# Seven places between the stages of a graph layer rearranged

## Chip, cores and metric

One Trainium2 chip; the kernel runs on 1 core. The metric is the device time in microseconds of one execution. An engine carries out its own instructions in order, and waits on semaphores for what the others deliver. The engines are TensorE (PE), VectorE (DVE), ScalarE (ACT) and GpSimd (POOL); SyncE (SP) issues most of the transfers.

## The reference

The input is 32 graphs of 512 nodes with 256 features, and an adjacency matrix for each. Cut to what matters:

```python
h = jnp.maximum(_layernorm(x, axis=-1), 0.0)
# the layer, on h:
c = relu(bn1(conv1d(hc, conv1_w)))                     # 1 tap, hc: h with channels in front
x_conv = relu(bn2(conv1d(c, conv2_w, pad 8)) + hc)     # 17 taps
s = h @ w_se.T + b_se                                  # 3 numbers a node
A = jnp.exp(-dist(s)) * adj
msg = relu(h @ w_msg.T + b_msg)
x_nmp = einsum('bnm,bmd->bnd', A, msg)
gi = concatenate([x_conv, x_nmp]) @ w_ih.T + b_ih
gh = h @ w_hh.T + b_hh
r, z = sigmoid(gi_r + gh_r), sigmoid(gi_z + gh_z)
nn_ = tanh(gi_n + r * gh_n)
out = x + (1 - z) * nn_ + z * h
```

## The kernel before, in words

All is float32. The 32 graphs are worked through in two groups of 16 (GB). For each group there are two stages, and after both groups a third runs over pairs of graphs. Almost everything stands under `tc.manual_schedule()`, where each engine gets its instructions in the order in which the program issues them; tiles in a few rotating buffers (`bufs=`) add the waits for a buffer.

**First stage** (`first_part`), once for each group, a loop over its graphs: load x (`load_x`), layer norm (`statistics`: bn_stats on DVE, the power of -1/2 on POOL, L398; `normalise`: four chunks of 128x256, L411 on DVE or L409 on ACT), transposes on PE into phT (L419) and relu into hT (L423), the first convolution (`conv1`, pc, L439; the bias is added on DVE into h, L442, relu on ACT, L443), and a transform of windows to a frequency-like domain (px, L454). In group 0 the weights of the second convolution are transformed in between (`weights_to_freq`, pw, L363; ACT or DVE copies them out to wst, SP stores them to wd). `between(b)` hands out these 32 transforms, two in an iteration, three in two of them (L1306). In group 1 the fronts of the loop carry the last four products of group 0, the `left` list (L1440 on), which `fill()` issues one entry at a time, and the sums that prepare the gates' weights (`combine`), whose first entry is a load of w_hhT by four transfers issued on POOL (L211).

**Node stage** (`nodes`), once for each group, a loop over the graphs in the order `todo`: 15, 14, 0, 1, ..., 13 in group 0. It has, for each graph, messages (`message`: products pm, L558, adds on DVE into st and msg, L560 and L561, relu on ACT, L565), features and their factors (`features`: fl and fr on ACT, L573 to L575; `factors`: two transposes psl and psr on PE, L580 and L584, copied by ACT to sl and sr, L582 and L587), exponents (`exponents`: pd, L604, exp on ACT, L610), the mask (`turn` transposes adj on DVE, L593; `masked`, L614), sums of blocks on POOL (`block_sums`, L641: ms, msg, ts, A, ms, ts, ms, ts) and the aggregation with seven products in place of eight (`aggregate7`, L666, adds on DVE at L680 to L686; `save_nmp` stores the result by SP). In between stand the products of the second convolution in the frequency domain, by units (`multiply(u)`, `product`, py, L503): re and im parts by PE, and for most units a third product of `both` (L483) and `wsum` (L470), which POOL prepares two units ahead (`prepare`; two buffers each). Group 0 has 36 units in its node stage over 16 graphs, so that an iteration has two or three (`mine`); the last has three: 33, 34 and 35. The last four units, 36 to 39, are the left-over ones.

**Third stage**, 16 pairs of graphs: `inverse` (back from the frequency domain, pc, L874, result in cp), gates r and z by 26 products with sums of operands (`gates_rz26`, pg, L911) and the third gate (`gate_n`, L928). The sums of operands are made by `block_sum` (L808 and L810) on POOL; for pair 0 they stand in `FIRST_ORDER`, the `hn` parts before `inverse(0)` and the `c` parts mixed in from index `ahead`, the first `c` entry. Only that one, ('t4', 'c'), is done by DVE; ('r5', 'c') follows it.

Of the kernel before, what the change touches and what calls it, by code (L numbers as in the profile page):

```python
# [12 lines left out]
AF = mybir.ActivationFunctionType  # L13
# [149 lines left out]
def gnn_layer(  # L163
# [15 lines left out]
    nc = tc.nc  # L179
# [5 lines left out]
    NC = N // P  # L185
    G = 3 * D
    W = N // V
    GB = P // W
# [44 lines left out]
    at, cols, n = {}, {}, 0  # L233
# [163 lines left out]
        nc.vector.tensor_scalar(rstd, mv[:, :, 1], LN_EPS, None, op0=ALU.add)  # L397
        nc.gpsimd.tensor_tensor(rstd, rstd, minus_half[:, :NC], op=ALU.pow)  # L398

    def normalise(b, by_scalar=False):  # L400
        mv, rstd = STATS.pop(b)
        XN[b] = pools["first"].tile([P, NC, D], FP, tag="xn", name=f"xn_{b}", bufs=2)
        if by_scalar:
            shift = work.tile([P, NC], FP, tag="shift", name=f"shift_{b}")
            nc.vector.scalar_tensor_tensor(shift, mv[:, :, 0], -1.0, rstd, op0=ALU.mult, op1=ALU.mult)
        for c in range(NC):
            dst, src = by_half(XN[b][:, c, :]), halves(X[b][:, c, :])
            if by_scalar:
                nc.scalar.activation(dst, src, AF.Identity, bias=shift[:, c : c + 1], scale=rstd[:, c : c + 1])  # L409
            else:  # L410
                nc.vector.tensor_scalar(dst, src, mv[:, c, 0:1], rstd[:, c : c + 1], op0=ALU.subtract, op1=ALU.mult)  # L411
        del X[b]
# [125 lines left out]
    def by_chunks(b):  # L538
        HQ[b] = work.tile([P, DC, N], FP, tag="hq", name=f"hq_{b}", bufs=2)
        for ic in range(DC):  # L540
            nc.scalar.copy(chunks(HQ[b][:, ic, :]), by_chunk(HT[b][:, ic, :]))
        del HT[b]

    SQ = {}

    def message(b, halves=range(2)):
        if 0 in halves:
            ST[b] = pools["nodes"].tile([P, NC, NS + 1], FP, tag="st", name=f"st_{b}", bufs=2)
            MSG[b] = pools["nodes"].tile([P, NC, D], FP, tag="msg", name=f"msg_{b}", bufs=3)
        hq = HQ[b]  # L550
        h = NC // 2
        for c0 in (h * k for k in halves):
            m = MSG[b][:, c0 : c0 + h, :]
            for j in range(h):
                c = c0 + j
                p = bank(f"pm_{b}_{c}")
                for ic in range(DC):
                    nc.tensor.matmul(p[:, : D + NS], hq[:, ic, c * P : (c + 1) * P], wmsg[:, ic, :],  # L558
                                     start=(ic == 0), stop=(ic == DC - 1))
                nc.vector.tensor_add(ST[b][:, c, :NS], p[:, D : D + NS], bmsg[:, D:])  # L560
                nc.vector.tensor_add(m[:, j, :], p[:, :D], bmsg[:, :D])  # L561
            if c0 > 0:
                SQ[b] = work.tile([P, NC, NS], FP, tag="sq", name=f"sq_{b}")
                nc.scalar.activation(SQ[b], ST[b][:, :, :NS], AF.Square)
            nc.scalar.activation(m, m, AF.Relu)  # L565
        if 1 in halves:
            del HQ[b]

# [222 lines left out]
    def block_sum(p, name, part):  # L791
        if name in BLOCK_SUMS:
            x, op, y = BLOCK_SUMS[name]
            dst, x, y = (operand(p, v, part) for v in (name, x, y))
            op = ALU.add if op == "+" else ALU.subtract
        else:
            rows = list(PAIR_SUMS)

            def whole(v):
                if isinstance(v, int):  # L800
                    return CP[p][:, v] if part == "c" else HN[p][:, :, v]
                return TNC[0][:, rows.index(v)] if part == "c" else TN[0][:, rows.index(v)]

            (x, y), op = PAIR_SUMS[name], ALU.subtract
            dst, x, y = whole(name), whole(x), whole(y)
            if part == "hn":
                for k in range(2):
                    nc.gpsimd.tensor_tensor(dst[:, k], x[:, k], y[:, k], op=op)  # L808
                return
        (nc.vector if (p, name, part) == (0, *FIRST_ORDER[ahead]) else nc.gpsimd).tensor_tensor(dst, x, y, op=op)  # L810

    def sums_ahead(p, part):
        for name in SUMS_AHEAD:
# [349 lines left out]
    def first_part(g, freq, between, left=()):  # L1163
# [15 lines left out]
            bn1_row(1, shift1, ones, diags)  # L1179
        if b0 not in STATS:  # L1180
            statistics(b0)
        normalise(b0)
        if g == 0:
            scale_w1()
            shift_w1()
# [11 lines left out]
        transpose_h(b0)  # L1197
        statistics(b0 + 1)
        fill()
        normalise(b0 + 1, g > 0)  # L1200
        if g > 0:
            statistics(b0 + 2)
        fill()
# [80 lines left out]
    with tc.tile_pool(name="freq", bufs=1) as fpool:  # L1284
# [3 lines left out]
        with phase("first", "gen"):  # L1288
            gen = pools["gen"]
            per = N // D  # L1290
            steps = [partial(weights_to_freq, gen, pc, i) for pc in range(QI // PI) for i in range(0, PI, per)]

            X[0] = pools["first"].tile([P, NC, D], FP, tag="x", name="x_0", bufs=3)
            for queue, c0, c1 in ((nc.sync, 0, 1), (nc.scalar, 1, 2), (nc.sync, 2, NC)):
                queue.dma_start(X[0][:, c0:c1, :], x[0, c0 * P : c1 * P, :].rearrange("(c p) d -> p c d", p=P))
            load_w1()
            load_x(1)
            load_taps(gen, 0, nc.sync)
            nc.sync.dma_start(taps, nc.inline_tensor(taps_np, name="dft_taps").ap())
            nc.sync.dma_start(fwd, nc.inline_tensor(fwd_np, name="dft_fwd").ap())  # L1300

            def between(b):
                if 1 <= b <= len(load_weights):
                    load_weights[b - 1]()

                n = (2, 0, *(3 if b in (6, 11) else 2 for b in range(2, GB)))[b]  # L1306
                mine = [[steps.pop(0)] for _ in range(n)]
                if b % 2 == 0 and b // 2 + 1 < QI // PI:
                    mine[b > 0].insert(0, partial(load_taps, gen, b // 2 + 1))
                return (mine[0], mine[1:]) if b == 0 else mine  # L1310

            with tc.manual_schedule():
                xf = first_part(0, freq_tile, between)
# [4 lines left out]
        def nodes(g, xf, units, last, following=()):  # L1318
# [29 lines left out]
            features(todo[0])  # L1348
            for step in message_sums(todo[0]):
                step()  # L1350
            message(todo[1], [0])
            factors(todo[0])
            by_chunks(todo[2])
            message(todo[1], [1])
            features(todo[1])
# [8 lines left out]
            for i, b in enumerate(todo):  # L1364
                mine = spread(units, i, last) if i < last else []
                more = todo[i + 1 : i + 5]
                seven = i <= last

                def bring():
                    if len(more) > 1:  # L1370
                        message(more[1])
                        features(more[1])

                def ahead():
                    if len(more) > 2:
                        load_adj(more[1], i % 2)
                    if len(more) > 3:
                        load_h(more[3])

                if len(more) == 2:  # L1380
                    load_adj(more[1], i % 2)
                flush()
                if g + 1 < NG and i == GB // 2:
                    load_x(b1)
                if g + 1 < NG and i == 3 * GB // 4:
                    statistics(b1)
                if i > 0:
                    ahead()
                if more:
                    factors(more[0])  # L1390
                if i == 0:
                    bring()
                for u in mine[:1]:
                    multiply(u)
                if i == 0:
                    ahead()
                if i > 0:
                    bring()
                if not seven:
                    aggregate(b, [0])  # L1400
                if more:
                    turn(more[0], [0, 1])
                    exponents(more[0])
                    masked(more[0], [0, 1])
                for u in mine[1:2]:
                    multiply(u)
                if more:
                    turn(more[0], [2, 3])
                    masked(more[0], [2, 3])
                if seven:  # L1410
                    aggregate7(b)
                else:
                    aggregate(b, [1])
                if len(more) > 2:
                    by_chunks(more[2])
                stores.append(partial(save_nmp, b))
                for u in mine[2:]:
                    multiply(u)
                if more and i + 1 <= last:
                    block_sums(more[0])  # L1420
            flush()

        with phase("pw", "ahead"):
# [3 lines left out]
            with phase("first", "sums"):  # L1427
                combine = combine_weights()

                def between(b):  # L1430

                    if b == GB - 3:
# [6 lines left out]
                pw, (u0, u1, u2, u3) = pools["pw"], range(UNITS - LEFT, UNITS)  # L1439
                left = [[partial(load_unit, 0, u2, pools["sums"]), partial(prepare, pw, 0, u1, xf)],  # L1440
                        [partial(product, pw, 0, u0, xf), partial(prepare, pw, 0, u2, xf)],
                        [partial(product, pw, 0, u1, xf), partial(load_unit, 0, u3), *combine.pop(0)],
                        [partial(prepare, pw, 0, u3, xf), partial(product, pw, 0, u2, xf)],
                        [partial(product, pw, 0, u3, xf)]]
                prepare(pw, 0, u0, xf)
                with tc.manual_schedule():
                    xf = first_part(1, freq_tile, between, left)
# [95 lines left out]
```

## Time and profile before

| | us |
|---|---|
| median of 3 runs | 1733.82 |
| all runs | 1733.5, 1733.82, 1737.73 |
| the profiled execution | 1737.52 |
| its span, first to last instruction | 1735.70 |

| stage | roughly, us of the span |
|---|---|
| first stage, group 0 | 0 to 161 |
| node stage, group 0 | 161 to 427 |
| first stage, group 1 | 427 to 544 |
| node stage, group 1 | 544 to 822 |
| third stage | 822 to 1736 |

A profile page gives, for each engine, its busy time and share of the span; a timeline gives start, duration, engine, line, operation and what it reads and writes, and in brackets how long the engine stood idle before and who released it. `128x512 f32` is partitions x elements. The chain of waits is the work that ended last, followed back. A wait listed as `PE py L503 <- POOL both L483` is one of PE at line 503 that ended when POOL had made `both`. In the table of stretches the columns are start and end, length, busy time (and instructions) of PE, its weight loads, DVE, ACT and POOL, then PE's granted clock, the transfers' share and GB/s.

### The profile page before, as it was taken

The numbers are of one execution on the slowest core, as the hardware profiler recorded it, in microseconds if no ns is written. First come the engines' busy times: TensorE is split into PE (matmuls) and PEld (weight loads), VectorE is DVE, ScalarE is ACT, GpSimd is POOL, SyncE is SP. The second block draws the span as 40 slices with busy tenths as digits, with TensorE's granted clock in tenths as the row PEclk, the third lists the DMA queues.
The fourth block names the chain that finished last, engine by engine and source line by source line (L and its number), as shares of the span: only waits on it lengthen the run. The fifth ranks groups of instructions, "written<-read, shape, count | busy, mean of one in ns | idle before, by whom it ended". The sixth has DMA issues, their size and how long they took to land.

```text
span 1735.7 us, 24321 instructions
## 1 busy us (share of the span) xinstructions
PE 1718.5 (99%) x7920; PEld 1323.0 (76%) x7920; DVE 1300.2 (75%) x2599; ACT 692.6 (40%) x1671; POOL 1086.8 (63%) x1071
## 2 busy tenths in 40 slices
PE   9999999999999999999999999999999999999998
PEld 6667888888898888886877787777877787778754
DVE  7785877777995667766587778777887788777867
ACT  4557555553446555554313232223223231323221
POOL 3341787777654677777767556765666556755551
PEclk9999999999999999999999999999999999999999
DMA  9988978975777988788523453245423552345323
GB/s 256 296 282 250 272 219 240 262 223 180 256 268 211 265 245 257 219 251 297 150 74 75 107 127 107 70 79 128 118 71 67 128 128 76 76 104 127 106 59 73
DMA packets 311682, 295.08 MB, mean 170 GB/s; under 512 B 147436, under 2 KB 241164, under 8 KB 311172
## 3 DMA queue, kind: packets, MB, share of 16 engines
q1 hardware_dynamic: 301588, 265.17, 55.7%
q0 software_dynamic: 6960, 26.65, 4.8%
q10 hardware_dynamic: 3008, 1.72, 0.3%
q8 instruction: 63, 1.03, 0.2%
q14 instruction: 63, 0.52, 0.1%
HBM read 194.31 MB, written 99.16 MB: 169 GB/s over the span
## 4 chain that ended last, share of the span: by engine, by line
PE 93%; DVE 2%; POOL 2%; DMA 1%; ACT 1%; SPq 1%; issue 1%; POOLq 0%; DVEq 0%; ACTq 0%
PE pg L911 29%; PE pn L928 17%; PE py L503 11%; PE pn L666 10%; PE pm L558 6%; PE pc L439 5%; PE px L454 3%; PE pc L874 3%; PE pd L604 2%; PE pw L363 2%; PE phT L419 1%; PE pg L928 1%; PE pz L928 1%; PE pc L877 1%; POOL tn L808 0%
## 5 line engine op out<-in xcount | busy, mean ns | idle before, releaser
L470 POOL TENSOR_TENSOR wsum<-wt 128x512 f32<-128x512 f32 x66 | 94.5, 1432 | 99.6 <-DMA wt<-wd 65.7
L503 PE MATMUL py<-wt,xf 128*128 128x256 f32 x640 | 154.2, 384 | 0.0
L911 PE MATMUL pg<-te,sw 128*128 128x256 f32 x600 | 154.0, 379 | 0.0
L902 ACT ACTIVATE rz<-rz,brz 128x256 f32<-128x256 f32 x180 | 86.4, 504 | 149.2 <-DVE rz L917 149.2
L503 PEld LDWEIGHTS py<-wt,xf 128*128 128x128 f32 x640 | 117.1, 190 | 34.9 <-issue 20.5
L911 PEld LDWEIGHTS pg<-te,sw 128*128 128x128 f32 x600 | 114.0, 190 | 15.5
L911 PE MATMUL pg<-hn,sw 128*128 128x256 f32 x480 | 123.2, 379 | 0.0
L911 PE MATMUL pg<-tn,sw 128*128 128x256 f32 x480 | 123.2, 379 | 0.0
L614 DVE TENSOR_TENSOR A<-A,at 128x512 f32<-128x512 f32 x124 | 116.2, 975 | 6.3 <-ACT A L610 2.7
L928 PE MATMUL pn<-tn,sw_n 128*128 128x512 f32 x256 | 120.3, 592 | 0.0
L439 PE MATMUL pc<-w,hT 128*128 128x256 f32 x512 | 119.2, 386 | 0.8 <-DVE hT L423 0.8
L1073 ACT ACTIVATE pn<-nt,vech 128x512 f32<-128x512 f32 x45 | 31.1, 692 | 217.8 <-DVE nt L1070 138.5
L558 PE MATMUL pm<-wmsg,hq 128*128 128x259 f32 x512 | 117.3, 381 | 0.0
L439 PEld LDWEIGHTS pc<-w,hT 128*128 128x128 f32 x512 | 95.9, 192 | 24.9 <-issue 8.0
L808 POOL TENSOR_TENSOR tn<-hn 128x512 f32<-128x512 f32 x64 | 86.2, 1367 | 35.7 <-PE pn L928 35.6
L558 PEld LDWEIGHTS pm<-wmsg,hq 128*128 128x128 f32 x512 | 96.6, 190 | 14.6
L911 PEld LDWEIGHTS pg<-hn,sw 128*128 128x128 f32 x480 | 91.1, 190 | 18.3 <-PE pn L928 3.3
L911 PEld LDWEIGHTS pg<-tn,sw 128*128 128x128 f32 x480 | 91.2, 190 | 12.4
L917 DVE TENSOR_TENSOR ct<-pg,ct 128x256 f32<-128x256 f32 x180 | 74.6, 415 | 32.9 <-PE pg L911 23.7
L398 POOL TENSOR_TENSOR rstd<-rstd,minus_half 128x4 f32<-128x4 f32 x32 | 33.3, 1042 | 103.0 <-DVE rstd L397 98.5
L928 PEld LDWEIGHTS pn<-tn,sw_n 128*128 128x128 f32 x256 | 48.6, 190 | 61.2 <-issue 50.5
L928 PE MATMUL pn<-hn,sw_n 128*128 128x512 f32 x192 | 90.3, 592 | 0.0
(232 smaller groups left out, 4385.4 us busy)
## 6 DMA issues: line engine op xcount, KB each, us to landing
wt<-wd SPq DMA_DIRECT2D x80, 512.0 KB, 6.3
adj<-in_adj_dram SPq DMA_DIRECT2D x128, 256.0 KB, 5.9
wd<-wst SPq DMA_DIRECT2D x64, 320.0 KB, 5.5
yd<-y SPq DMA_DIRECT2D x76, 256.0 KB, 5.0
hd<-hT SPq DMA_DIRECT2D x32, 512.0 KB, 4.4
nd<-nmp SPq DMA_DIRECT2D x32, 512.0 KB, 2.9
xb<-in_x_dram SPq DMA_DIRECT2D x128, 128.0 KB, 6.0
out_dram<-xb SPq DMA_DIRECT2D x122, 128.0 KB, 2.8
```

Source lines behind the costliest of these rows:

```text
L439: nc.tensor.matmul(p[:, j, :], HT[b][:, ic, c * P : (c + 1) * P], w1[:, ic, :], start=(ic == 0), stop=(ic == DC - 1))
L454: nc.tensor.matmul(p[:, j * 2 * L : (j + 1) * 2 * L], H1[b][:, c0 + j, ic * P : (ic + 1) * P], fwd, start=True, stop=True)
L470: nc.gpsimd.tensor_tensor(t, WT[g, u][:, 0], WT[g, u][:, 1], op=ALU.add)
L503: nc.tensor.matmul(dst, v[:, ic, :], w[:, ic, :], start=(ic == 0), stop=(ic == DC - 1))
L558: nc.tensor.matmul(p[:, : D + NS], hq[:, ic, c * P : (c + 1) * P], wmsg[:, ic, :], start=(ic == 0), stop=(ic == DC - 1))
L614: nc.vector.tensor_mul(A[b][:, mc, :], EXP.pop((b, mc)), AT.pop((b, mc)))
L666: nc.tensor.matmul(bk, left[:, k, :], right[:, k, :], start=(first and k == 0), stop=(k == 1), skip_group_check=True)
L808: nc.gpsimd.tensor_tensor(dst[:, k], x[:, k], y[:, k], op=op)
L902: nc.scalar.activation(at(dst), at(src), AF.Sigmoid, bias=brz[:, o : o + 1], scale=sign)
L911: nc.tensor.matmul(bk, SW["hk"][:, k, s, :], c if k == 2 else hn[:, k], start=(onto is None and k == 0), stop=(k == K3 - 1), skip_group_ch ...
L917: nc.vector.tensor_tensor(at(dst), at(x), at(y), op=op)
L928: nc.tensor.matmul(bk[:, t], weight(q, k, o), terms[k][q][:, t], start=(first and i == 0), stop=(i == len(ks) - 1), skip_group_check=True)
```

## The change

Seven places, all of them an order or an engine; no arithmetic is changed.

1. `normalise` takes a list of chunks for ACT instead of yes or no. Graph 0 (the first of group 0) gives it chunks 2 and 3; group 1 gives all, as before, where it gave all.
2. `between` in group 0: the iterations with a third weight transform are 12 and 14 instead of 6 and 11.
3. At the head of `nodes`, the relu of the first half of the second graph's messages is issued after the factors of the first graph.
4. In the first iteration of `nodes`, the first half of the third graph's messages is issued before `factors` of the second graph (its relu with it); second half and features after.
5. In the last iteration of `nodes`, the third unit's products come before `aggregate7` instead of after. Only group 0 has units there.
6. `left`: the load of w_hhT goes from the third entry to the last.
7. `block_sum`: DVE does the first two `c` sums of pair 0 instead of one.

```diff
@@ -397,7 +397,7 @@
         nc.vector.tensor_scalar(rstd, mv[:, :, 1], LN_EPS, None, op0=ALU.add)
         nc.gpsimd.tensor_tensor(rstd, rstd, minus_half[:, :NC], op=ALU.pow)
 
-    def normalise(b, by_scalar=False):
+    def normalise(b, by_scalar=()):
         mv, rstd = STATS.pop(b)
         XN[b] = pools["first"].tile([P, NC, D], FP, tag="xn", name=f"xn_{b}", bufs=2)
         if by_scalar:
@@ -405,7 +405,7 @@
             nc.vector.scalar_tensor_tensor(shift, mv[:, :, 0], -1.0, rstd, op0=ALU.mult, op1=ALU.mult)
         for c in range(NC):
             dst, src = by_half(XN[b][:, c, :]), halves(X[b][:, c, :])
-            if by_scalar:
+            if c in by_scalar:
                 nc.scalar.activation(dst, src, AF.Identity, bias=shift[:, c : c + 1], scale=rstd[:, c : c + 1])
             else:
                 nc.vector.tensor_scalar(dst, src, mv[:, c, 0:1], rstd[:, c : c + 1], op0=ALU.subtract, op1=ALU.mult)
@@ -543,7 +543,7 @@
 
     SQ = {}
 
-    def message(b, halves=range(2)):
+    def message(b, halves=range(2), later=None):
         if 0 in halves:
             ST[b] = pools["nodes"].tile([P, NC, NS + 1], FP, tag="st", name=f"st_{b}", bufs=2)
             MSG[b] = pools["nodes"].tile([P, NC, D], FP, tag="msg", name=f"msg_{b}", bufs=3)
@@ -562,7 +562,11 @@
             if c0 > 0:
                 SQ[b] = work.tile([P, NC, NS], FP, tag="sq", name=f"sq_{b}")
                 nc.scalar.activation(SQ[b], ST[b][:, :, :NS], AF.Square)
-            nc.scalar.activation(m, m, AF.Relu)
+            relu = partial(nc.scalar.activation, m, m, AF.Relu)
+            if later is None:
+                relu()
+            else:
+                later.append(relu)
         if 1 in halves:
             del HQ[b]
 
@@ -807,7 +811,7 @@
                 for k in range(2):
                     nc.gpsimd.tensor_tensor(dst[:, k], x[:, k], y[:, k], op=op)
                 return
-        (nc.vector if (p, name, part) == (0, *FIRST_ORDER[ahead]) else nc.gpsimd).tensor_tensor(dst, x, y, op=op)
+        (nc.vector if p == 0 and (name, part) in FIRST_ORDER[ahead : ahead + 2] else nc.gpsimd).tensor_tensor(dst, x, y, op=op)
 
     def sums_ahead(p, part):
         for name in SUMS_AHEAD:
@@ -1179,7 +1183,7 @@
             bn1_row(1, shift1, ones, diags)
         if b0 not in STATS:
             statistics(b0)
-        normalise(b0)
+        normalise(b0, range(2, NC) if g == 0 else ())
         if g == 0:
             scale_w1()
             shift_w1()
@@ -1197,7 +1201,7 @@
         transpose_h(b0)
         statistics(b0 + 1)
         fill()
-        normalise(b0 + 1, g > 0)
+        normalise(b0 + 1, range(NC) if g > 0 else ())
         if g > 0:
             statistics(b0 + 2)
         fill()
@@ -1303,7 +1307,7 @@
                 if 1 <= b <= len(load_weights):
                     load_weights[b - 1]()
 
-                n = (2, 0, *(3 if b in (6, 11) else 2 for b in range(2, GB)))[b]
+                n = (2, 0, *(3 if b in (12, 14) else 2 for b in range(2, GB)))[b]
                 mine = [[steps.pop(0)] for _ in range(n)]
                 if b % 2 == 0 and b // 2 + 1 < QI // PI:
                     mine[b > 0].insert(0, partial(load_taps, gen, b // 2 + 1))
@@ -1348,8 +1352,11 @@
             features(todo[0])
             for step in message_sums(todo[0]):
                 step()
-            message(todo[1], [0])
+            relus = []
+            message(todo[1], [0], relus)
             factors(todo[0])
+            for relu in relus:
+                relu()
             by_chunks(todo[2])
             message(todo[1], [1])
             features(todo[1])
@@ -1386,10 +1393,13 @@
                     statistics(b1)
                 if i > 0:
                     ahead()
+                if i == 0:
+                    message(more[1], [0])
                 if more:
                     factors(more[0])
                 if i == 0:
-                    bring()
+                    message(more[1], [1])
+                    features(more[1])
                 for u in mine[:1]:
                     multiply(u)
                 if i == 0:
@@ -1407,6 +1417,10 @@
                 if more:
                     turn(more[0], [2, 3])
                     masked(more[0], [2, 3])
+                if not more:
+                    for u in mine[2:]:
+                        multiply(u)
+                    mine = mine[:2]
                 if seven:
                     aggregate7(b)
                 else:
@@ -1439,9 +1453,9 @@
                 pw, (u0, u1, u2, u3) = pools["pw"], range(UNITS - LEFT, UNITS)
                 left = [[partial(load_unit, 0, u2, pools["sums"]), partial(prepare, pw, 0, u1, xf)],
                         [partial(product, pw, 0, u0, xf), partial(prepare, pw, 0, u2, xf)],
-                        [partial(product, pw, 0, u1, xf), partial(load_unit, 0, u3), *combine.pop(0)],
+                        [partial(product, pw, 0, u1, xf), partial(load_unit, 0, u3)],
                         [partial(prepare, pw, 0, u3, xf), partial(product, pw, 0, u2, xf)],
-                        [partial(product, pw, 0, u3, xf)]]
+                        [partial(product, pw, 0, u3, xf), *combine.pop(0)]]
                 prepare(pw, 0, u0, xf)
                 with tc.manual_schedule():
                     xf = first_part(1, freq_tile, between, left)
```

## The prediction

> **What bounds the kernel now.** I read the engine totals first, then TensorE's own waits, then the order of time at three seams between stages.
>
> ```profile
> PE 1718.5 (99%) x7920; PEld 1323.0 (76%) x7920; DVE 1300.2 (75%) x2599; ACT 692.6 (40%) x1671; POOL 1086.8 (63%) x1071
> ...
> PE py L503 <- POOL both L483: 2.0, 1, 2.0
> PE pn L666 <- POOL ts L641: 0.8, 1, 0.8
> PE psl L580 <- ACT fl L573: 0.7, 2, 0.3
> PE pd L604 <- DVE msg L561: 0.5, 1, 0.5
> PE pd L604 <- ACT sr L587: 0.5, 1, 0.5
> PE pg L911 <- POOL tnc L810: 0.3, 1, 0.3
> ```
>
> TensorE (PE) is busy 99% of the span: 1735.7-1718.5 = 17.2 us in all are not. No product is added or removed, so a gain is at most the waits listed (total us, times, longest), and a loss is a new PE wait, which nothing later gives back: the products queue behind it. The second seam, aggregation of the last graph of group 0, PE then GpSimd (POOL) in order of time, and one step of the chain of waits:
>
> ```profile
> 415.11 1.89 PE L503 MATMUL py<-wt,xf 128*128 128x256 f32 x8
> 416.84 1.03 PE L503 MATMUL py<-wsum,both 128*128 128x256 f32 x4
> 417.70 2.03 PE L666 MATMUL pn<-A,msg 128*128 128x256 f32 x8
> 420.51 1.13 PE L666 MATMUL pn<-ts,ms 128*128 128x256 f32 x4 [0.78 <-POOL ts L641]
> ...
> 424.93 1.89 PE L503 MATMUL py<-wt,xf 128*128 128x256 f32 x8
> ...
> 427.52 1.16 PE L419 MATMUL phT<-ident,xn 128*128 128x128 f32 x8
> ...
> 421.10 1.27 POOL L641 TENSOR_TENSOR ts<-A,ts 128x512 f32<-128x512 f32 x1
> 422.33 1.45 POOL L470 TENSOR_TENSOR wsum<-wt 128x512 f32<-128x512 f32 x1
> ...
> 424.46 0.87 POOL both L483
> ```
>
> POOL runs from 400.15 to 426.7 without a pause: block sums of the last graph first, then wsum and both of unit 35. The second `both` starts at 424.46, so unit 35's ended there. Third, the front of the node stage, ScalarE (ACT), then VectorE (DVE):
>
> ```profile
> 172.66 0.32 ACT L582 COPY sl<-psl 128x128 f32<-128x128 f32 x1
> 172.81 1.22 ACT L587 ACTIVATE sr<-psr,mask 128x128 f32<-128x128 f32 x4
> 176.50 0.63 ACT L565 ACTIVATE msg<-msg 128x512 f32<-128x512 f32 x1 [2.48 <-DVE msg L561]
> ...
> 173.84 1.83 DVE L614 TENSOR_TENSOR A<-A,at 128x512 f32<-128x512 f32 x2
> 175.60 0.15 DVE L560 TENSOR_TENSOR st<-pm,bmsg 128x3 f32<-128x3 f32 x1
> ```
>
> Today ACT makes sl and sr long before the third graph's message relu, which stands idle 2.48 us for DVE.
>
> ```profile
> 74.00:76.00 2.00, 2.00 (x14) 1.48 (x12) 2.00 (x6) 1.31 (x4) 0.00 (x0) 0.60 0.96 244
> 76.00:78.00 2.00, 2.00 (x10) 0.42 (x9) 1.97 (x9) 0.04 (x1) 1.10 (x2) 0.50 1.03 408
> ```
>
> The column after the engines is PE's granted clock: it falls to half for 6.83 us from 74.39. Three rows there took 1.82, 2.01 and 5.36 us where their like took 1.04, 1.10 and 3.72: 3.33 us lost. The profiled execution took 1737.52 us (span 1735.70 and 1.82 around it); the runs are 1733.5, 1733.82 and 1737.73. The stretch seems to be in some executions and not in others, so I add edits to the median, 1733.82; against the profiled time the sum is 3.7 higher.
>
> **Edit 1, loop fronts (places 3 and 4 of the change; twice, groups 0 and 1).** Moving the second graph's first relu behind sr frees sr 1.04 us earlier (sl could start at 166.51, when psl is done, not 167.55). pd then starts when PE is free, 168.22 (psl at 166.24, two small products 0.22, eight pm products 1.75), not 168.89. The hq copies behind it come 1.04-0.54 = 0.5 earlier, and so do the square, DVE's reduction and its masked products. Putting the third graph's first half ahead of `factors` fills the wait for fl (0.33). But its relu now stands on ACT ahead of sl and sr of the second graph. That relu needs DVE adds which stand behind all four masked products: they end at 175.67-0.5 = 175.17, two pairs of adds take 0.80 and the last add's tail 0.07, relu starts at 176.04, sl at 176.58, sr at 176.73 and, at 1.22, ends at 177.95. PE comes to pd at 174.75 (168.22 + 1.07 pd + 0.22 + 3.50 pm + 1.73 py) and stands 3.2 us; pd starts at 178.0 instead of 176.42: +1.55. What is queued behind on ACT (square, exps of that graph) ends about 1 us later, but DVE waits there till 180.19 for adj anyway. Group 1: relu 559.38-0.5 = 558.88, sr's end 558.88+0.54+0.15+1.22 = 560.79, pd 560.83 instead of 559.88: +0.95. Together **+2.5**; from -2.0 (the relu delays nothing, 1.0 won per group) to +3.5 (DVE isn't earlier).
>
> **Edit 2, last aggregation (place 5).** Unit 35's products now precede the seven products; POOL's order stays. PE starts at 417.70, finishes re and im at 419.43, and the third product needs wsum and both: 424.50, **5.07 us idle**. That product after a wait takes 0.97 (444.47 to 445.44), the 28 matmuls 6.04: 431.51, where PE was at 427.52. Also, unit 35 (2.59) was the cover under which DVE finished the graph's adds and normalised the next one; now phT follows at once. Last add 431.54 to 431.95, four xn at the undisturbed 1.38 of 7.23: 433.3; phT ends near 433.9 instead of 428.52: +5.4. SyncE stores nmp before it loads the next x, so x comes 5.8 later too.
>
> **Edit 3, left-over products (place 6).** POOL's four w DMAs (2.19) now come behind wsum and both of unit 39. The x load goes ahead of them, and the w load lands some 8 us later, before the combine steps that want it two graphs on. After edit 2: x of graph 18 is issued at about 433.3 (429.51 before), lands by 440.2, statistics and rstd end by 444.15, then x issue 0.80, wsum 1.27, both 0.73: 446.95. PE wants it at 447.8. The 1.97 wait is gone; xn (DVE, 447.1 to 448.5) is just in time for phT at 448.65. The convolution of graph 17 then starts at 449.5 instead of 446.31: edits 2 and 3 together **+3.2**; bounds +2.0 (3.99-1.97, the cover not missed) and +5.4 (no gain from edit 3, the chain through x being as late as PE).
>
> **Edits 4 to 6 (places 2, 7 and 1).** Third transforms go from graphs 6 and 11 to 12 and 14. At graph 6 the wait of 0.40 at 70.41 is for DVE's h, late through rstd on POOL behind the loaded vectors, and stays; 0.32 at 72.14 was the moved transform's own: **-0.2**, bounds -0.5 and +0.5. First gates: r5's `c` sum (POOL 831.77, 1.27) goes to DVE, idle 828.12 to 833.89; ready at 829.0, PE doesn't wait (0.33, and 0.11 of restart): **-0.5**, bounds -0.5 and 0; POOL's later sums come 1.27 earlier, and cover nobody. First normalisation: two of four xn (0.33 each) to ACT (0.52 each, idle then; the same function at 435.78 brings no table load), a shift of 0.1 added: **-0.3**, bounds -0.6 and +0.3.
>
> Sum: 2.5+3.2-0.2-0.5-0.3 = **+4.7**, 1738.5.
>
> **The clock.** The window before the drop at 74.39 held only waits of 0.40 and 0.32 besides transforms and phT. One with 5 us of nothing is emptier, so I expect the half-clock stretch after edit 2's wait in most executions (chance 0.7), at 3.3 at most: 1741.8. The Trainium skill (TensorE: Matmul & The Clock Gate, Why this matters for your kernels) advises no idle gaps beyond about 3 us, else half clock. That speaks against this change (5.07 and 3.2 us); without the drop the sum is 1738.5, with it 1741.8, with one more at the first front 1745.1. The drop at 74.39 shows less than such a gap doing it. I forecast **1741**.
>
> **Rivals.** (a) Faster: POOL hands over unit 35's sums before 419.4. Then all waits go: 2.0+0.8+0.7+1.0+0.3 and 0.9 of edits 4 and 6, 5.7 us: 1728.1. It decides if POOL's order were other than the code's; the rows show it in one queue, 5 us late. 0.07. (b) Same: the waits come and the clock holds, 1738.5, or edit 1's relu is in time too (-2.0 for +2.5), 1734.0. For it: the 1.97 wait at 442.5 brought no drop. Against it: that wait is less than half as long. 0.30. (c) My case, 1741.8, and with a second drop, at the first front's 3.2 us, 1741.8+3.3 = 1745.1: 0.63.
>
> 0.3% is 5.2 us, about what a measurement here can tell from none: faster is below 1728.6, slower above 1739.0. The range 1734 to 1746 leaves out (a) and, above, all bounds high with two drops.
>
> **What would show it.** In the changed kernel: a PE wait of 5 us for `both` at L503 ahead of the last seven products; phT L419 waiting for xn; pd waiting 2.7 to 3.2 us for sr in each group; none for both at the left-over products; none for tnc; a half-clock stretch near 425 to 434. I am wrong if POOL's unit 35 sums precede the block sums, or if ACT's sr comes before that relu.

## The result, and the profile after

The changed kernel takes 1747.40 us (median of 6 runs, 1745.48 to 1749.5) where the kernel before, on the same chip, takes 1734.73 (6 runs): ratio 1.0069, 95% interval 1.0056 to 1.0082. On a second chip, later, it took 1747.29 against 1735.98 (ratio 1.0062, 1.0047 to 1.0078). The change costs 11 to 13 us; the forecast, 1741 on a base of 1733.82, has 7.2.

TensorE (PE) has no work added, and the waits of the changed kernel show what it stands for. The view of PE's waits, after (engine, line and tile; releaser; us in total, times, longest):

```profile
PE pd L608 <- ACT sr L591: 5.7, 2, 3.4
PE py L503 <- POOL both L483: 4.7, 1, 4.7
PE phT L419 <- DVE xn L411: 2.0, 2, 1.1
PE row L1180 <- DVE fr L329: 1.5, 1, 1.5
```

Of before's list, the 2.0 us for `both` at the left-over products, the 0.8 for `ts`, the 0.7 for `fl` and the 1.0 ahead of pd are gone; 5.7 for `sr` and 4.7 for unit 35's `both` are new. That is 10.4 new against 4.5 gone; the wait of `phT` for `xn` grew besides, from 0.6 to 2.0. Some 6 to 7 us net, then, a little more than half of what was lost. The rest is in the next view, windows of PE (from:to, length, then busy us and records of PE, weight load, DVE, ACT, POOL; then granted clock, transfer share, GB/s), after. Each pair is a stretch and the one behind it:

```profile
7.28:10.69 3.41, 1.95 (x12) 1.09 (x11) 2.31 (x7) 1.75 (x4) 0.83 (x1) 1.00 1.09 130
10.69:14.10 3.41, 3.41 (x8) 2.71 (x9) 2.25 (x11) 0.19 (x1) 1.69 (x2) 0.50 1.03 312
174.50:177.95 3.45, 0.30 (x3) 0.30 (x5) 2.20 (x10) 2.18 (x8) 2.71 (x3) 1.00 1.21 220
177.95:181.36 3.41, 3.41 (x11) 1.70 (x9) 1.29 (x3) 3.05 (x10) 3.33 (x3) 0.50 1.07 298
423.70:427.12 3.42, 0.00 (x0) 0.00 (x0) 0.00 (x0) 0.00 (x0) 3.42 (x4) 1.00 0.57 220
427.12:430.53 3.41, 3.24 (x8) 2.62 (x9) 0.42 (x1) 0.00 (x0) 3.04 (x4) 0.50 0.00 0
567.00:570.48 3.48, 1.63 (x9) 0.87 (x10) 2.21 (x7) 3.48 (x14) 3.24 (x4) 1.00 0.72 218
570.48:573.89 3.41, 3.41 (x9) 2.70 (x9) 2.33 (x2) 1.87 (x5) 2.18 (x2) 0.50 1.26 224
```

Before's profile had one stretch at half clock, of 6.83 us. After's has four, of 3.41 us, and three of them stand directly behind the three new waits. (The last 3 to 7 us of every trace here are at half clock too; they are left out of what follows.) Work that runs at half rate for 3.41 us has lost 1.7 us.

The three waits themselves, each in the order of time (start, duration, engine, line, what; in brackets the idle time before and its releaser). First front, PE (the first two lines before, the others after):

```profile
174.60 1.89 PE L503 MATMUL py<-wt,xf 128*128 128x256 f32 x8
176.42 1.14 PE L604 MATMUL pd<-sr,sl 32*128 32x512 f32 x8
...
172.32 1.89 PE L503 MATMUL py<-wt,xf 128*128 128x256 f32 x8
177.65 2.40 PE L608 MATMUL pd<-sr,sl 32*128 32x512 f32 x8 [3.44 <-ACT sr L591]
179.98 2.66 PE L503 MATMUL py<-wt,xf 128*128 128x256 f32 x8
```

And ACT at that time, after:

```profile
175.77 0.63 ACT L567 ACTIVATE msg<-msg 128x512 f32<-128x512 f32 x1 [4.29 <-DVE msg L561]
176.31 0.25 ACT L586 COPY sl<-psl 128x128 f32<-128x128 f32 x1
176.45 1.15 ACT L591 ACTIVATE sr<-psr,mask 128x128 f32<-128x128 f32 x4
```

`sl` and `sr` need nothing but their transposes, which PE had made by 170.7; they stand on ACT behind the third graph's relu, which waits 4.29 us for DVE. pd then takes 2.40 us where the eight records of pd just before it, at 167.42, took 1.14, and the py behind it 2.66 instead of 1.89. Some 0.3 us of that is the start after a wait (such a pd takes 1.45 at full clock, in the filled kernel below); the rest is the half clock. The crossing, PE and POOL, after:

```profile
420.66 1.89 PE L503 MATMUL py<-wt,xf 128*128 128x256 f32 x8
427.29 2.08 PE L503 MATMUL py<-wsum,both 128*128 128x256 f32 x4 [4.74 <-POOL both L483]
429.16 2.57 PE L670 MATMUL pn<-A,msg 128*128 128x256 f32 x8
...
436.98 1.64 PE L419 MATMUL phT<-ident,xn 128*128 128x128 f32 x8 [0.93 <-DVE xn L411]
...
424.08 1.26 POOL L645 TENSOR_TENSOR ts<-A,ts 128x512 f32<-128x512 f32 x1
425.30 1.26 POOL L470 TENSOR_TENSOR wsum<-wt 128x512 f32<-128x512 f32 x1
426.52 1.40 POOL L483 TENSOR_TENSOR both<-xf 128x256 f32<-128x256 f32 x2
```

POOL's order is before's: the block sums of the last graph, then `wsum`, then `both` (the row counts units 35's and the next one's). PE wants the third product at 422.5 and gets it at 427.3. The second front, in group 1, PE, after:

```profile
564.68 1.89 PE L503 MATMUL py<-wt,xf 128*128 128x256 f32 x8
568.85 1.45 PE L608 MATMUL pd<-sr,sl 32*128 32x512 f32 x8 [2.29 <-ACT sr L591]
570.23 3.58 PE L503 MATMUL py<-wt,xf 128*128 128x256 f32 x8
```

Here pd still runs at full clock; the clock falls at 570.48, and the py takes 3.58 us.

Where the time went, by landmarks of PE (starts of named products in each trace, the differences worked out; "fill" and "best" are experiments below):

| stretch of PE's program | before | after | after, again | fill | best |
|---|---|---|---|---|---|
| start to the first message product | 160.98 | 160.10 | 157.09 | 156.80 | 157.41 |
| first front, to the first pn | 19.21 | 23.24 | 23.33 | 21.67 | 18.86 |
| aggregations and crossing, to graph 17's convolution | 266.12 | 270.97 | 270.99 | 269.53 | 264.53 |
| to the first pn of group 1 (second front in it) | 117.33 | 120.30 | 120.33 | 119.16 | 116.70 |
| to the first gate stage | 258.22 | 258.21 | 258.22 | 258.22 | 258.21 |
| first gates | 38.97 | 38.38 | 38.38 | 38.38 | 38.38 |
| to the end | 874.91 | 876.52 | 875.96 | 875.07 | 876.85 |

(The row of the first gates has the first `inverse` in it.) The first and the last row move by up to 4 and 2 us between these executions; the first holds a half-clock stretch in before and in the first execution of after. The rows between them repeat within 0.1 us in the two executions of the changed kernel; in two other pairs of runs with the same order of work there (before and place 1 alone, best with and without place 1) they differ by up to 0.8. They carry the change: in the second execution +4.1, +4.9, +3.0 and -0.6 against before, together +11.4 (11.3 in the first).

### The profile page after: what moved, and what is told of

It reads as the page before. It is cut to its first block, busy times and chain, and to the rows that moved or that the text cites. A ratio compares the mean times of both kernels' runs of the same rounds, so it can differ in the third digit from the quotient of the medians.

```text
span 1747.7 us, 24318 instructions
## 1 busy us (share of the span) xinstructions
PE 1722.4 (99%) x7920; PEld 1325.5 (76%) x7920; DVE 1298.5 (74%) x2599; ACT 693.8 (40%) x1673; POOL 1081.2 (62%) x1070
## 3 DMA queue, kind: packets, MB, share of 16 engines
q8 instruction: 63, 1.03, 0.2%
## 4 chain that ended last, share of the span: by engine, by line
PE 73%; DVE 1%; POOL 1%; issue 0%; ACT 0%; DMA 0%; SPq 0%; DVEq 0%; POOLq 0%
PE pg L915 29%; PE pn L932 15%; PE py L503 6%; PE pn L670 5%; PE pc L878 3%; PE pc L439 3%; PE pm L558 3%; PE px L454 2%; PE pd L608 1%; PE phT L419 1%; PE pz L932 1%; PE pg L932 1%; PE pc L881 1%; PE pn L653 1%; POOL sw_last L844 0%
```

## The experiments

### One part at a time, on the kernel before

**Place 1 alone** (graph 0's chunks 2 and 3 normalised on ACT). The trace after had stood 2.4 us late from graph 1 on.

```diff
...
-        normalise(b0)
+        normalise(b0, range(2, NC) if g == 0 else ())
```

> The kernel before with place 1 alone (chunks 2 and 3 of graph 0's normalisation on ACT). Theory: the whole change's trace stood 2.4 us late after the start, but for a reason that has nothing to do with place 1 (graph 0's load landed about 0.9 us later there, and the clock dropped in another slice); place 1 alone then gives -0.6 to +0.3 us. Rival: place 1 itself makes the wait at the first transposes and the drop of the clock from 10.7 us on; then +2 to +2.5 us, in every run, and the trace has the half clock at 10.7 to 14.1 us again.

Measured: 1735.72 us against 1736.75, ratio 0.9995 (0.9986 to 1.0004). The rival's 2 us in every run are not there. The profiled execution did have a half-clock stretch in the start, but at another place: from 17.8 us on, behind waits at graph 1's transposes (0.59 us) and products (1.03), and not at 10.7 behind graph 0's. Of eight profiled executions with place 1 in this study two have such a stretch in the first 25 us, of five without it none has. That is too few to acquit place 1 of a small share, and enough to say that the late start of the first trace is no fixed part of the 12 us: the second execution of the same kernel comes to its first message product 3.0 us sooner.

**Places 3 and 4 alone**, the loop fronts.

```diff
...
-            message(todo[1], [0])
+            relus = []
+            message(todo[1], [0], relus)
             factors(todo[0])
+            for relu in relus:
+                relu()
...
+                if i == 0:
+                    message(more[1], [0])
                 if more:
                     factors(more[0])
                 if i == 0:
-                    bring()
+                    message(more[1], [1])
+                    features(more[1])
```

> The kernel before with places 3 and 4 alone (the loop fronts). Theory: the third graph's relu stands on ACT ahead of sl and sr, pd waits 3.4 us (graph group 0) and 2.3 us (group 1) for sr, and after each of these waits the clock is halved for 3.41 us, which costs some 1.65 us each: +6 to +7 us in all, of which +2.5 to +3.6 is waiting. Rival 1, the clock does not follow the wait: +2.5 to +3.6 us. Rival 2, place 4 gains because the factors come behind one half of the message only: -2 us.

Measured: 1743.01 against 1736.75, ratio 1.0041 (1.0027 to 1.0055), +6.3 us. pd waits 2.77 and 2.3 us for `sr`, and the trace has two stretches at half clock, one behind each wait, and no other. Both rivals miss: 2.5 to 3.6 us without the clock is below the interval (4.7 to 9.6 us), a gain further off.

**Place 5 alone**, the third unit ahead of the last aggregation.

```diff
+                if not more:
+                    for u in mine[2:]:
+                        multiply(u)
+                    mine = mine[:2]
                 if seven:
                     aggregate7(b)
```

> The kernel before with place 5 alone (the last iteration's third unit ahead of the last aggregation). Theory: k3 of unit 35 waits 4.7 us for both, since POOL makes the affinity's sums and wsum first; the clock is then halved for 3.41 us (1.6 us), the later phT waits some 1 to 2 us for xn, and the wait of 2 us at the left-over products stays: +4 to +6.5 us. Rival: the unit's products cover the wait that the aggregation had, and the rest is nothing: -1 to +0.5 us.

Measured: 1742.18 against 1736.75, ratio 1.0031 (1.0019 to 1.0043), +5.4 us, as the theory has it. Here the clock stays low for two windows, 6.83 us. Windows of this kernel (columns as above):

```profile
416.00:418.00 2.00, 0.41 (x2) 0.01 (x1) 0.42 (x1) 0.66 (x2) 2.00 (x4) 1.00 0.99 361
418.00:420.00 2.00, 0.00 (x0) 0.00 (x0) 0.00 (x0) 0.00 (x0) 2.00 (x2) 1.00 0.76 293
420.00:422.00 2.00, 0.86 (x2) 0.77 (x3) 0.00 (x0) 0.00 (x0) 2.00 (x4) 0.51 0.00 0
422.00:424.00 2.00, 2.00 (x6) 1.55 (x6) 0.42 (x1) 0.00 (x0) 1.64 (x2) 0.50 0.00 0
424.00:426.00 2.00, 2.00 (x7) 1.55 (x6) 0.00 (x0) 0.37 (x1) 1.30 (x2) 0.50 0.34 131
426.00:428.00 2.00, 2.00 (x9) 1.69 (x8) 0.00 (x0) 0.66 (x2) 0.00 (x0) 0.78 0.04 8
```

The clock falls at 420.0, still inside the wait (it ends at 421.14). The first low window is then a third idle, and full rate returns only at 426.9, after a second one that is full of products.

**Places 2, 6 and 7 alone.**

```diff
-                n = (2, 0, *(3 if b in (6, 11) else 2 for b in range(2, GB)))[b]
+                n = (2, 0, *(3 if b in (12, 14) else 2 for b in range(2, GB)))[b]
...
-        (nc.vector if (p, name, part) == (0, *FIRST_ORDER[ahead]) else nc.gpsimd).tensor_tensor(dst, x, y, op=op)
+        (nc.vector if p == 0 and (name, part) in FIRST_ORDER[ahead : ahead + 2] else nc.gpsimd).tensor_tensor(dst, x, y, op=op)
...
-                        [partial(product, pw, 0, u1, xf), partial(load_unit, 0, u3), *combine.pop(0)],
+                        [partial(product, pw, 0, u1, xf), partial(load_unit, 0, u3)],
...
-                        [partial(product, pw, 0, u3, xf)]]
+                        [partial(product, pw, 0, u3, xf), *combine.pop(0)]]
```

> The kernel before with places 2, 6 and 7 alone (third transforms, left-over products, first gates). Theory: -0.2 for the transforms, -0.5 for the gates, and -2.0 if the wait at the left-over products goes when w_hhT's load comes later: -1.5 to -2.7 us. Rival: the wait of 2.0 us moves to the next product or transpose: -0.7 to 0 us. The four parts together should come to the whole change's +12.7 us within 2 us; a larger gap means that the parts act on each other.

Measured: 1735.39 against 1736.75, ratio 0.9991 (0.9982 to 1.0), -1.4 us, at the weak end of the theory; its interval takes in nothing as well. The wait for `both` at the left-over products is gone from the list and no new one came, and the first gates take 38.38 us instead of 38.97. By the landmarks of its trace the crossing takes 264.50 us, 0.9 to 1.6 less than in the two runs with before's order there (265.39 and 266.12). The four parts come to +0.58%, with their intervals some 0.23% either way; the whole measured 0.69 and 0.62%. Within that they add up.

### Repairs on the changed kernel

**The relu of place 4 behind the factors**, as place 3 has it.

```diff
                 if i == 0:
-                    message(more[1], [0])
+                    message(more[1], [0], relus := [])
                 if more:
                     factors(more[0])
                 if i == 0:
+                    for relu in relus:
+                        relu()
                     message(more[1], [1])
```

> The changed kernel, with the third graph's first relu issued on ACT behind sl and sr, as place 3 already does for the second graph. Theory: sl and sr no longer stand behind a relu that waits for DVE, both waits of pd (3.44 and 2.29 us) go to under 0.6 each, and with them the two stretches at half clock behind them (1.7 us each): 6 to 9 us less than the changed kernel, which is +4 to +7 us against the kernel before. Rival: the wait only changes its name, because DVE's four adds of the message are late for the second half too, or pd then waits for fl and fr; less than 3 us gained, +10 us or more against before.

Measured: 1739.16 against 1735.81, ratio 1.0018 (1.0008 to 1.0028), +3.4 us, 8 to 9 less than the changed kernel, where 6 to 9 were forecast. PE's waits of this version:

```profile
PE py L503 <- POOL both L483: 4.7, 1, 4.7
PE phT L419 <- DVE xn L411: 2.2, 2, 1.2
PE row L1180 <- DVE fr L329: 1.5, 1, 1.5
PE pd L608 <- DVE msg L561: 1.0, 1, 1.0
```

No wait for `sr` is left, though pd now waits 1.0 us for the message in the first front (under 0.6 was forecast), and of the clock's falls in the trace only that of the crossing is left. The two fronts, each from its first message product to its first pn, take 19.96 and 17.88 us, where before takes 19.21 for each and the changed kernel 23.24 and 22.15. One relu ahead of two copies was the whole loss at the fronts.

**Unit 35's two sums on DVE.**

```diff
-        nc.gpsimd.tensor_tensor(t, WT[g, u][:, 0], WT[g, u][:, 1], op=ALU.add)
+        (nc.vector if (g, u) == (0, 35) else nc.gpsimd).tensor_tensor(t, WT[g, u][:, 0], WT[g, u][:, 1], op=ALU.add)
...
-            nc.gpsimd.tensor_tensor(both, re, im, op=ALU.add)
+            (nc.vector if (g, u) == (0, 35) else nc.gpsimd).tensor_tensor(both, re, im, op=ALU.add)
```

> The changed kernel, with unit 35's wsum and both added on DVE instead of POOL. Theory: the wait of 4.74 us at k3 is POOL's queue alone (the last graph's affinity sums stand ahead of the two), so it goes to under 1 us, and the half clock behind it (1.7 us) with it; DVE has the room: 4.5 to 6.5 us less than the changed kernel, +6 to +8 us against before. Rival 1: the unit waits for something else at the same time (its weights' transfer, xf), and the wait keeps over 3 us under another name. Rival 2: DVE's two operations delay xn, and the later waits at phT grow by what is gained: +11 us or more.

Measured: 1742.38 against 1735.81, ratio 1.0037 (1.0023 to 1.0052), +6.6 us. The wait of 4.74 us is gone, so it was POOL's queue; but a part of it stands further on. PE in this version:

```profile
421.30 1.89 PE L670 MATMUL pn<-A,msg 128*128 128x256 f32 x8
...
426.48 1.03 PE L670 MATMUL pn<-ts,msg 128*128 128x256 f32 x4
429.55 2.21 PE L419 MATMUL phT<-ident,xn 128*128 128x128 f32 x8 [2.04 <-DVE xn L411]
431.55 2.72 PE L503 MATMUL py<-wt,xf 128*128 128x256 f32 x8
```

The transposes now wait 2.04 us for `xn` (0.93 in the changed kernel), and 2.72 us for a py of 1.89 tell of the half clock behind that. With unit 35 moved ahead, nothing covers the time in which DVE finishes the aggregation and normalises the next graph. Place 5 doesn't pay even with its first wait repaired: from the first pn to graph 17's convolution this version takes 266.56 us (447.95 less 181.39), and without place 5 it is 264.53 (the version called best below); by the two rows some 1.4 us of that is the half clock (2.21 and 2.72 us against 1.64 and 1.89).

**Unread products in the waits.** To part the clock from the wait, PE was given something to do while the same tiles came at the same time.

```diff
         pd = [bank(f"pd_{b}_{mc}") for mc in range(NC)]
+        for _ in range({14: 12, 30: 7}.get(b, 0)):
+            nc.tensor.matmul(pd[0][:, :D], ident, wmsg[:, 0, :D], start=True, stop=True)
...
         for dst, v, w in terms:
+            for _ in range(18 if (g, u) == (0, 35) and dst is not k1 and dst is not k2 else 0):
+                nc.tensor.matmul(dst, ident, wmsg[:, 0, :D], start=True, stop=True)
```

> The changed kernel, with products that nobody reads (identity by w_msg, 128x256) put where PE waits: 12 ahead of the first pd and 7 ahead of the second, in the bank that pd starts anew, and 18 ahead of unit 35's k3, in k3's bank. At 0.236 us each by the rows of py they fill 2.8, 1.7 and 4.2 us of waits of 3.44, 2.29 and 4.74 us, so every tile comes when it did. Theory: the half clock follows from PE standing without products; the three stretches at 0.5 go, and with them 3 x 1.7 = 5 us: +7 to +8.5 us against before. Rival: the clock falls for another reason (power, the transfers, the time since the last fall), the three stretches stay and the time is the changed kernel's or above it by up to 2 us: +12 to +15 us against before.

Measured: 1745.92 against 1735.81, ratio 1.0056 (1.0044 to 1.0069), +10.1 us: neither forecast. The profile tells why. The rows of the fills are 5.34, 3.19 and 7.93 us long: the trace keeps two records for each of these products, and one product takes 0.43 us, not 0.236. The fills overran the waits by up to 3 us and moved the tiles' users. The clock, though, stayed at 1.00 up to the last 5 us. A second try had half as many (6, 4 and 9), run beside the changed kernel.

> The changed kernel once more, beside the two that follow, on one chip. Theory: the three waits come again with at least one stretch at half clock behind each, and the parts add up: +9 to +13.5 us against before (the four parts measured by themselves give 0.58%, about +10 us). Rival: the parts act on each other, and the whole costs more than their sum in every run: +14 us or more.

> The changed kernel with unread products in PE's three waits, now sized by the trace of the first try, where one such product took 0.43 us and not 0.236 (its row counts two records for one product): 6 ahead of the first pd, 4 ahead of the second, 9 ahead of k3, which is 2.6, 1.7 and 3.9 us in waits of 3.44, 2.29 and 4.74 us. Theory: the tiles come when they did, the three stretches at half clock do not come, and 3 x 1.7 us (more where a stretch lasted 6.83 us) are gained: 4 to 7 us less than the changed kernel beside it, +4 to +8 us against before. Rival: the half clock costs little in the end, because the work behind it waits for other engines anyway: within 2 us of the changed kernel beside it.

Measured: the changed kernel 1747.29, the filled one 1742.21 (ratio to before 1.0032, 1.0021 to 1.0043), before 1735.98. The filled kernel does more work and is 5.1 us faster by the medians, where 3 x 1.7 would be 5.1; either median is sure to 2 to 3 us only. By the landmarks its trace is 1.7 us faster in the first front, 1.5 in the crossing and 1.6 in the second front (20.56 us against 22.16 from its first message product), 4.7 in all. PE in it:

```profile
170.75 2.75 PE L609 MATMUL pd<-wmsg,ident 128*128 128x256 f32 x12
174.40 1.45 PE L612 MATMUL pd<-sr,sl 32*128 32x512 f32 x8 [0.90 <-ACT sr L593]
175.78 1.99 PE L505 MATMUL py<-wt,xf 128*128 128x256 f32 x8
...
417.52 4.05 PE L503 MATMUL py<-wmsg,ident 128*128 128x256 f32 x18
422.42 1.13 PE L505 MATMUL py<-wsum,both 128*128 128x256 f32 x4 [0.85 <-POOL both L483]
```

`sr` and `both` come as late as ever: 0.90 and 0.85 us of waiting are left behind the fills, and pd starts 17.60 us after the first message product (17.64 in the changed kernel beside it). py takes 1.99 us instead of 2.66, and the trace has no half-clock stretch up to its last 4 us. This settles that the half clock follows PE's empty time, and what a stretch costs, 1.5 to 1.7 us. The remaining +6.2 us are the waits, less what the other places gain.

### A version that beats both

Places 2, 3, 4, 6 and 7, with the relu of place 4 behind the factors as in the diff above; without places 1 and 5. And the same with place 1.

> The kernel before with places 2, 3, 4, 6 and 7, the relu of place 4 behind sl and sr, and without places 1 and 5. Theory: the fronts with the relu behind the factors cost nothing or gain up to 2 us (the factors start after one half of the message), places 2, 6 and 7 gave -1.4 us: -1 to -4 us against before, below the kernel before in most runs. Rival: the split message costs PE a wait for the second half's st, or features come later: 0 to +3 us.

> The faster version (places 2, 3, 4, 6, 7 with the second relu behind the factors) with place 1 added, so that only place 5 and the place of one relu tell it from the changed kernel. Theory: place 1 is worth -0.6 to +0.3 us by itself, and the half clock at the start comes by chance with or without it: -2 to -4.5 us against before. Rival: place 1 makes the start late, 2 us, where a wait at the first transposes is followed by the half clock: -1 to +1 us against before.

Measured: 1732.94 against 1735.81, ratio 0.9980 (0.9971 to 0.9989), 2.9 us less than before and below it with its whole interval; with place 1 1733.30 against 1735.98, ratio 0.9988 (0.9977 to 0.9999). The two can't be told apart. ACT in the first:

```profile
168.62 0.32 ACT L586 COPY sl<-psl 128x128 f32<-128x128 f32 x1
168.77 1.22 ACT L591 ACTIVATE sr<-psr,mask 128x128 f32<-128x128 f32 x4
172.90 0.63 ACT L1402 ACTIVATE msg<-msg 128x512 f32<-128x512 f32 x1 [2.91 <-DVE msg L561]
```

The relu still waits for DVE, 2.91 us, but nothing that PE needs stands behind it. The first front takes 18.86 us (19.34 with place 1, 19.21 before), the second 17.88 (17.89 with place 1, 19.21 before), and the trace has no half-clock stretch up to its last 6 us. With the relu out of the way, the fronts' gain is the 1.3 us of the second.

## Why the prediction was right or wrong

**The base.** The edits were added to 1733.82, the median of three runs. Beside the result before took 1734.73 (6 runs), and over the 69 runs beside the experiments, on three chips, the medians are 1736.75, 1735.81 and 1735.98: the base was 1 to 3 us low.

**Edit 1, loop fronts.** The mechanism is the one described: the relu ahead of `sl` and `sr`, waits of 3.44 and 2.29 us, gone when the relu is moved. The size was wrong. Without the clock (the filled kernel) the fronts cost +2.5 and +1.4, 3.8 together, where +2.5 was forecast and +3.5 was the upper bound. In the first, DVE was to be 0.5 us earlier, and lost that waiting 0.51 us for the adjacency's transfer at 169.33. In the second the wait came as worked out: pd starts 16.40 us after the front's first message product, and 15.45 before, which is the +0.95 forecast. What no term held is that pd takes longer after a wait: from its start to the first pn it is 4.07 and 4.16 us in the filled kernel, and 3.77 and 3.76 before.

**Edit 2, last aggregation.** Right: a wait of 5.07 us was worked out, 4.74 came, from POOL's block sums. The fear that phT loses its cover was right in kind and mild here, 0.93 us; the run with DVE's sums shows it at 2.04.

**Edit 3, left-over products.** Right in the wait: the 2.0 us are gone, alone and in the whole. One time on the way to it doesn't fit: edit 2 has x 5.8 us later, and edit 3 goes on with 433.3, which is 3.8 later than 429.51. The trace has 5.8 (that x is issued at 438.49, in a program whose first pn stands 3.15 later), and the wait went all the same. Edits 2 and 3 together were put at +3.2; the filled kernel shows +3.4 for that stretch.

**Edits 4 to 6.** First gates -0.6 against -0.5. Third transforms and first normalisation lie in the start, which moves by more from run to run than the -0.2 and -0.3 forecast; they are not resolved.

**The clock**, the step that failed most. It was given one half-clock stretch, behind the crossing, with chance 0.7 and 3.3 us at most, and a second one, at the first front, only as a variant of the same case; nothing was put behind the second front's wait. There are three, one behind each wait, the 2.29 us one included, in both profiles of the changed kernel; without them the time falls by 4.7 us (rows) to 5.1 (medians). The argument that before's wait of 1.97 us had brought no fall didn't reach far: 2.29 us was enough. The price of one was also read from a stretch twice as long (3.3 for 6.83 us; 1.5 to 1.7 for 3.41), so that the variant's two stretches, at 6.6 us, were put above what the three took. That 1745.1 comes so near is luck.

The sum by the rows: fronts +3.8, crossing with the left-over products +3.4, first gates -0.6, the clock +4.7, together 11.3; the table has 11.4, and 1735.98 + 11.4 is 1747.4, where 1747.29 was measured on that chip. Forecast were 1733.8, +4.7 for the edits and +2.5 for the clock. The errors of the base (0.9 and 2.2 on the two chips where the changed kernel ran), the edits (1.5 to 2) and the clock (2.2 to 2.6) all point the same way, and no one of them alone makes up the 6.4 us.

**The rivals.** (a), POOL handing unit 35 over in time, fell with the 4.74 us. (b), the clock holding, is what the filled kernel shows; in the unfilled one the clock falls three times.

The page of the Trainium skill that was weighed (TensorE: Matmul & The Clock Gate, Why this matters for your kernels) warns of idle gaps beyond about 3 us. It was right for the two longer waits (3.44 and 4.74 us) and not strict enough for the third (2.29 us).

## What to carry to other kernels

Where one engine is busy 99% of the time, look for what is issued ahead of its operands in another engine's queue: one relu that waits for a third engine, put before two small copies, cost 8 to 9 us, more than all the gains of the change. Count a long wait of TensorE twice: the wait, and what a stretch at half clock behind it costs, here 1.5 to 1.7 us for 3.41 us and 3.3 for 6.83. In these traces every wait of TensorE of 2.04 us or more brought one. Single waits of 1.97 and 1.54 us did not, but several of 0.3 to 1.1 us close together in the start did, in two executions. And before a product is moved ahead as useful work, ask what it covered where it stood.

## What the hardware showed

The half clock comes in whole steps of 3.41 us, on a grid that stands anywhere against the program. Laid over that grid, the traces of twelve executions sort by how long PE was busy in a window. (The first 4 to 8 us, for which the trace has no clock, and the last 10 or so, in which PE's work ends, are left out.) All fourteen windows with 1.63 us or less were followed by half rate, one of them at half rate itself. Of eight with 1.87 to 2.19 us two were (1.95 and 2.10 us) and six weren't. Of those entered at full rate with more, one alone was followed by half rate, before's at 70.98 with 3.09 us busy; what sets that one apart stays open. Three windows already at half rate, with 2.31, 2.73 and 3.41 us busy, were followed by a second one at half rate, the others by full rate; what decides there is open too. Nor is 1.63 us a sharp limit: in the tail of the changed kernel's first trace a window with 1.60 us busy (from 1737.84) was followed by full rate. So what a wait costs seems to depend on how the grid cuts it: before's wait of 1.97 us, cut in two by the grid, left windows of 2.9 and 1.97 us busy and cost nothing more, while 2.29 us in one window left 1.63 and did. If 1.63 us held everywhere, any wait of 3.6 us (2 x (3.41 - 1.63)) would bring the clock down however it is cut; that is worked out, not tried.
